# A macaron transformer block on one core: the turn between attention and the second feed-forward part, with its score steps in pairs, and the last statistics at other steps

## The chip, the cores and the metric

The kernel runs on one core of a Trainium2 chip. The metric is the device time of one execution in microseconds (us), as the median of the runs shown. A profile is one further execution, recorded by the hardware; its clock starts at the start of its span.

The engines are PE (TensorE, matmuls and transposes), PEld (its weight loads), DVE (VectorE), ACT (ScalarE), POOL (GpSimd) and SP (SyncE, here only DMA issues). Each works through its own list in order.

## The reference: what is computed

The input is 16 sequences of 256 tokens with 256 features, in float32. Three parts follow one another, each on a layernorm of x and added to x:

```
x = x + 0.5 * ffn(layernorm(x))       # 256 -> 1024, exact gelu, 1024 -> 256, weights
                                      # rounded to -1, 0, 1 by the mean of their sizes
x = x + attn(layernorm(x))            # 16 heads of 16 features, rotary, causal softmax
x = x + 0.5 * ffn(layernorm(x))       # the same weights as in the first part
```

## The kernel before

**Feed-forward.** x stays on the chip as eight blocks of 512 tokens (`xs[0..7]`, four tiles of 128 tokens each; sequence b is tiles 2b and 2b+1, so block b // 2). `ffn` (line 273) makes a part with `ln` = 0 or 2. Its unit is a step (`step`, line 373), of which there are 8 for each block i, one for each f of 128 hidden features, and `LATE` = 2 more at the end. A step u = 8i + f does `up(i, f)`: four matmuls from `xnT` into a PSUM tile "m" (`up_first`, unless made earlier), two gelus on ACT (`h_high`, rounded, and `h_whole`), and their difference `h_rest`, which POOL makes for f = 1, 3, 5 and DVE for the others. Then it does `down` for the step two earlier: eight matmuls with `h_high` and `h_rest` into a PSUM tile "w". At f = 3 DVE normalizes the next block (`prepare`, not for i = 0 of the last part), at f = 5 and 6 that is transposed (`turn_in`: four transposes into a PSUM tile "mm", a copy on ACT to the rounded half of `xnT`, a subtraction on DVE for the other half), and at f = 6 POOL adds the output bias to the block (`add_bias`). After f = 7's `down`, DVE adds the result to x, and SP stores the block.

**Attention.** A sequence b goes through eight slots p of two heads each. `scores` (line 505) makes scores in two forms: those of the sequence before, keys by queries, into a tile "w" (they become probabilities), and those of the current one, queries by keys, into tiles "m" or "w", from which DVE takes each row's maximum. A head uses 32 rows of PE's array, rows 32 * (h % 4), so the two heads of a slot take two of its four row groups; the other form uses slot p ^ 1 and so the other two. `scores` returns `weigh` (line 557): DVE adds the causal mask to "w", and ACT makes `pT`, its exp. `attend` multiplies four groups of heads by the values, ACT copies the result to `avs`; `divide` transposes that and divides by the sums on DVE (`o`); `turn_out` transposes `o` and copies it (`oT`); `project_out` multiplies by the output weights; `add_out` adds to x on DVE; `last_stats` (line 640) makes the layernorm statistics of the sequence's two tiles: four instructions on DVE (`st`, `mv`, twice) and two on POOL (`var`, `rstd`). `turn_max` transposes the maxima, copies them (`mT`) and sends them into `qT` by two DMAs of SP.

**The turn** (lines 745 to 797) is what the change touches. Sequences 13, 14 (called a) and 15 (z) are then still on their way: the scores of z have to be made, without other scores beside them, and the first two blocks of the last part are made ready at the same time. `prepare(1, gpsimd)` normalizes block 1 on POOL, `turn_in(1, 0)` and `turn_in(1, 1)` transpose it, and four `up_first` of block 0 run early. What remains of z (`tail`) stands behind the first steps of the last part, one item after each step.

**What sets the order.** All instructions of an engine run in the order in which the program issues them (`InOrder`, line 159; so every instruction of the compute engines shows line 167 in the profile). The order is written out by hand: `ahead` is issued between a slot's scores and its `weigh`, `behind` after it. PSUM is divided into three pools of two buffers each: "w" (two banks a buffer, one slot's scores of two heads), "m" and "mm" (one bank each). All transposes, `attend`, `project_out` and the projections use "mm".

Of the kernel before, what the change touches and what calls it, by code (L numbers as in the profile page):

```python
# [19 lines left out]
NFC = FF // P  # L20
# [9 lines left out]
def kernel(  # L30
# [15 lines left out]
    NB = NT // S  # L46
# [54 lines left out]
    for k in range(KC):  # L101
        rows = slice(k * P, (k + 1) * P)
        nc.sync.dma_start(out=wv[:, k, :], in_=wqkvT[rows, 2 * D :])
        for at in range(0, 2 * D, 4 * HD):
            n, j, e = at // D, at // P % 2, at // (4 * HD) % 2
# [53 lines left out]
    class InOrder:  # L159
# [11 lines left out]
    tensor, vector, scalar, gpsimd, sync = (  # L171
        InOrder(engine) for engine in (nc.tensor, nc.vector, nc.scalar, nc.gpsimd, nc.sync)
    )
# [4 lines left out]
    def stats(ln, n):  # L178
        st = small.tile([P, 6], FP, name="st")
        vector.bn_stats(st, tokens(n))  # L180
        vector.bn_aggr(mv[ln][:, n, :], st)
# [312 lines left out]
    def turn_max(b, j):  # L494

        tp = ps_mm.tile([P, S], FP, name="mm")
        for c in range(2):
            tensor.transpose(tp[:, c * P : (c + 1) * P], maxes[b % 2][:, c, j, :], ident)
        mT = hp.tile([P, S], FP, name="mT")
        scalar.copy(mT, tp)  # L500
        for e in range(2):
            rows = slice(HD * (1 - e), P, 32)
            sync.dma_start(out=qT[b][rows, 2 * j + e, :], in_=mT[rows, :])

    def scores(bw, pw, bm, pm):

        w = m = None  # L510
        if bw is not None:
            w = ps_w.tile([P, 2, 512], FP, name="w")
        if bm is not None and bw is None:
            both = ps_w.tile([P, 2, 512], FP, name="w")
            m = [both[:, j, :] for j in range(2)]
        elif bm is not None:
            m = [ps_m.tile([P, 512], FP, name="m") for j in range(2)]
        for c in range(2):
            for j in range(2):
                if w is not None:  # L520
                    h = 2 * pw + j
                    rows, g = slice(32 * (h % 4), 32 * (h % 4) + 32), h // 4
                    tensor.matmul(
                        w[:, j, c * S : S + c * P],
                        kT[bw][rows, g, c * P : (c + 1) * P],
                        qT[bw][rows, g, c * P : S],
                        start=(c == 0),
                        stop=(c == 1),
                    )
                if m is not None:  # L530
                    h = 2 * pm + j
                    rows, g = slice(32 * (h % 4), 32 * (h % 4) + 32), h // 4
                    tensor.matmul(
                        m[j][:, c * P : c * P + (c + 1) * P],
                        qT[bm][rows, g, c * P : (c + 1) * P],
                        kT[bm][rows, g, 0 : (c + 1) * P],
                        start=(c == 0),
                        stop=(c == 1),
                    )
        if m is not None:  # L540
            for j in range(2):
                h = 2 * pm + j
                at = 32 * (h % 4) + HD * (1 - h // 4 % 2)
                for c in range(2):
                    cols = (c + 1) * P
                    vector.tensor_tensor_reduce(
                        out=pp.tile([P, S], FP, name="masked")[:, 0:cols],
                        in0=m[j][:, c * P : c * P + cols],
                        in1=mask_q[:, S - cols : S],
                        scale=-1.0,  # L550
                        scalar=-MASKED,
                        op0=ALU.add,
                        op1=ALU.min,
                        accum_out=maxes[bm % 2][:, c, h // 8, at : at + 1],
                    )

        def weigh():

            at = w.rearrange("p h (d w) -> p h d w", w=2 * P)[:, :, :, 0:P]
            mask = mask_k.unsqueeze(1).unsqueeze(1).to_broadcast([P, 2, 2, P])  # L560
            vector.tensor_add(at, at, mask)

            pT[bw, pw] = prp.tile([P, 2, S + P], FP, name="pT")
            scalar.activation(pT[bw, pw], w[:, :, 0 : S + P], AF.Exp, scale=HD**-0.5)

        return weigh if w is not None else lambda: None

    def attend(b, half, take=True):


        av = ps_mm.tile([P, 2, S], FP, name="mm")
        for n in range(2):
            g = 2 * half + n
            for c in range(2):
                for r in range(4):
                    tensor.matmul(
                        av[32 * r : 32 * r + 32, n, c * P : S],
                        vals[b % 2][:, c, 4 * g + r, :],
                        pT[b, 2 * g + r // 2][:, r % 2, c * S : S + c * P],
                        start=(c == 0),  # L580
                        stop=(c == 1),
                    )
        sums[b, half] = av
        if take:
            take_sums(b, half)

    def take_sums(b, half):
        av, sums[b, half] = sums[b, half], pp.tile([P, 2, S], FP, name="avs")
        scalar.copy(sums[b, half], av)

    def divide(b, half):

        if half == 0:
            o[b] = pp.tile([P, 2, H, HD], FP, name="o")
        tp = ps_mm.tile([P, 2, 8, 32], FP, name="mm")
        for c in range(2):
            for n in range(2):
                tensor.transpose(
                    tp[:, c, 4 * n : 4 * n + 4, :].rearrange("p h d -> p (h d)"),
                    sums[b, half][:, n, c * P : (c + 1) * P],  # L600
                    ident,
                )
        inv = pp.tile([P, 2, 8, 1], FP, name="inv")
        vector.reciprocal(inv, tp[:, :, :, HD : HD + 1])
        vector.tensor_mul(
            o[b][:, :, 8 * half : 8 * half + 8, :],
            tp[:, :, :, 0:HD],
            inv.to_broadcast([P, 2, 8, HD]),
        )

    def turn_out(b):
        tp = ps_mm.tile([P, KC, S], FP, name="mm")
        for k in range(KC):
            for c in range(2):
                tensor.transpose(
                    tp[:, k, c * P : (c + 1) * P],
                    o[b][:, c, 8 * k : 8 * k + 8, :].rearrange("p h d -> p (h d)"),
                    ident,
                )
        oT[b] = pp.tile([P, KC, S], FP, name="oT")  # L620
        scalar.copy(oT[b], tp)

    def project_out(b):
        y = y_a[b] = ps_mm.tile([P, 2, D], FP, name="mm")
        for c in range(2):
            for k in range(KC):
                tensor.matmul(
                    y[:, c, :],
                    oT[b][:, k, c * P : (c + 1) * P],
                    wo[:, k, :],  # L630
                    start=(k == 0),
                    stop=(k == KC - 1),
                )

    def add_out(b):
        at = 2 * b % BT
        xt = xs[2 * b // BT][:, at : at + 2, :]
        vector.tensor_add(xt, y_a[b], xt)

    def last_stats(b):  # L640
        for c in range(2):
            stats(2, 2 * b + c)
        finish_stats(2, 2 * b, 2)
# [101 lines left out]
    begin, step, prepare, turn_in, up_first = ffn(2, store)  # L745
    rest = []
    for p in range(8):
        made = []
# [9 lines left out]
    a, z = NB - 2, NB - 1  # L758


    ahead = {
        0: lambda: project_out(NB - 3),
        1: lambda: turn_max(z, 1),
    }
    behind = {
        0: lambda: (add_out(NB - 3), prepare(1, gpsimd)),
        2: lambda: attend(a, 1),
        3: lambda: (up_first(0, 0), made.append(turn_in(1, 0))),
        4: lambda: (made.pop()(), divide(a, 1), up_first(0, 1)),
        5: lambda: (turn_out(a), made.append(turn_in(1, 1))),  # L770
        6: lambda: (made.pop()(), attend(z, 0)),
        7: lambda: (project_out(a), divide(z, 0), add_out(a)),
    }
    for p in range(8):
        weigh = scores(z, p, None, None)
        ahead.get(p, lambda: None)()
        weigh()
        behind.get(p, lambda: None)()

    more = ps_w.tile([P, 2, TB], FP, name="w")  # L780
    for f in range(2):
        up_first(0, 2 + f, more[:, f, :])
    tail = [
        lambda: attend(z, 1, False),
        lambda: take_sums(z, 1),
        lambda: divide(z, 1),
        lambda: turn_out(z),
        lambda: project_out(z),
        lambda: add_out(z),
        lambda: last_stats(NB - 3),  # L790
        lambda: last_stats(a),
        lambda: last_stats(z),
    ]
    for u in range(FFN_STEPS):
        step(u)
        if u < len(tail):
            tail[u]()
# [49 lines left out]
```

## Time and profile before

| | us |
|---|---|
| median of three runs | 623.5 (623.47 to 624.73) |
| the profiled execution | 623.6 |
| its span | 621.8 |
| PE busy | 600.7 (97%) |
| DVE busy | 462.1 (74%) |
| ACT busy | 415.3 (67%) |
| POOL busy | 306.4 (49%) |
| the turn, from the end of slot 7 of z to attend(z, 1) | 466.3 to 487.9 |
| the last feed-forward part behind it | to 621.8 |

The granted clock of PE was 0.998 of full speed. Lines of the timeline give the start, the duration, the engine, the operation with its tiles (output<-inputs) and shapes, and in brackets the idle time of the engine before it and who ended it. Equal neighbours are merged (x4). Matmuls are pipelined: the ends of PE's rows are modelled, and starts tell more. A matmul in float32 leaves two records.

### The profile page before, as it was taken

The page shows a single profiled execution, that of the slowest core. Times are in us where ns is not written, and L with a number is a line of the kernel's source. Part 1 is how long each engine was busy: PE and PEld are TensorE (multiplying, and loading weights), DVE is VectorE, ACT ScalarE, POOL GpSimd, SP SyncE. Part 2 cuts the span into 40 slices and gives each one's busy share as a digit, 9 for nine tenths or more (in the row PEclk, how much of TensorE's full clock was granted, in tenths as well). Part 3 has the DMA queues.
Part 4 walks back from the last instruction along what each step waited for, and adds up shares of the span by engine and source line. Part 5 has one row for each costly group of instructions (what it writes and reads, how often), then busy time and mean ns, then how long its engine had stood idle before and what let it go on. Part 6 is the DMA issues. An engine that isn't in the chain of part 4 may idle for free.

```text
span 621.8 us, 14721 instructions
## 1 busy us (share of the span) xinstructions
PE 600.7 (97%) x5580; PEld 487.5 (78%) x5580; DVE 462.1 (74%) x1650; ACT 415.3 (67%) x716; POOL 306.4 (49%) x277
## 2 busy tenths in 40 slices
PE   4999999999999999999999999999999999999997
PEld 3798999887667777777777777777766788888886
DVE  6877777785788888888888888888885375555553
ACT  4666766674576667776777677767765666676674
POOL 3655555782464455545564456553442163334443
PEclk9999999999999999999999999999999999999999
DMA  9800000000001000110010001100100011011001
GB/s 286 178 21 1 2 1 18 17 1 18 20 35 38 18 22 35 37 36 21 19 37 36 20 20 36 37 19 21 36 4 2 1 35 35 34 35 35 26 21 56
DMA packets 25478, 21.30 MB, mean 34 GB/s; under 512 B 10944, under 2 KB 21056, under 8 KB 25408
## 3 DMA queue, kind: packets, MB, share of 16 engines
q1 hardware_dynamic: 24848, 19.44, 9.9%
q8 instruction: 44, 0.72, 0.5%
q10 hardware_dynamic: 560, 0.92, 0.4%
q14 instruction: 26, 0.21, 0.1%
HBM read 7.51 MB, written 4.19 MB: 19 GB/s over the span
## 4 chain that ended last, share of the span: by engine, by line
PE 87%; DVE 7%; ACT 2%; issue 2%; POOL 1%; DMA 1%; DVEq 0%; ACTq 0%; POOLq 0%
PE mm L167 37%; PE w L167 28%; PE m L167 21%; DVE h_rest L167 2%; DVE st L167 1%; DVE xn L167 1%; ACT h_high L167 1%; ACT h_whole L167 1%; DVE w2q L167 1%; DMA x<-in_x_dram 1%; DVE mv L167 1%; DVE masked L167 0%; DVE x L167 0%; POOL h_rest L167 0%; POOL rstd L167 0%
## 5 line engine op out<-in xcount | busy, mean ns | idle before, releaser
L167 DVE CUSTOM_DVE_ANT_0 masked<-m,mask_q 128x128 f32<-128x128 f32 x480 | 142.7, 353 | 41.0 <-PE m L167 39.7
L167 PE MATMUL m<-xnT,w1q 128*128 128x512 f32 x504 | 142.5, 404 | 0.9 <-DVE w1q L167 0.9
L167 ACT ACTIVATE h_high<-m,b_sb 128x512 fp32r<-128x512 f32 x126 | 86.7, 688 | 79.2 <-PE m L167 79.2
L167 DVE TENSOR_TENSOR h_rest<-h_whole,h_high 128x512 fp32r<-128x512 f32 x83 | 76.1, 918 | 71.0 <-ACT h_whole L167 70.6
L167 ACT ACTIVATE pT<-w 128x768 f32<-128x768 f32 x128 | 104.1, 814 | 31.6 <-DVE w L167 24.6
L167 PE MATMUL w<-qT,kT 32*128 32x256 f32 (+1 forms) x1024 | 121.7, 349 | 0.8 <-ACT pT L167 0.5
L167 POOL TENSOR_TENSOR h_rest<-h_whole,h_high 128x512 fp32r<-128x512 f32 x45 | 60.3, 1340 | 125.7 <-ACT h_whole L167 125.5
L167 PE MATMUL w<-w2q,h_high 128*128 128x256 f32 x480 | 120.9, 286 | 1.1 <-DVE w2q L167 1.1
L167 PE MATMUL w<-w2q,h_rest 128*128 128x256 f32 x480 | 118.0, 280 | 1.3 <-POOL h_rest L167 1.2
L167 PEld LDWEIGHTS w<-qT,kT 32*128 32x128 f32 x1024 | 90.7, 184 | 32.4 <-issue 26.4
L167 PE MATMUL m<-kT,qT 32*128 32x128 f32 x960 | 114.9, 349 | 0.7 <-ACT kT L167 0.7
L167 PEld LDWEIGHTS m<-xnT,w1q 128*128 128x128 f32 x504 | 86.7, 190 | 16.4 <-DVE xnT L167 2.9
L167 PEld LDWEIGHTS w<-w2q,h_rest 128*128 128x128 f32 x480 | 90.6, 189 | 6.4 <-POOL h_rest L167 1.8
L167 PEld LDWEIGHTS w<-w2q,h_high 128*128 128x128 f32 x480 | 90.4, 188 | 5.8 <-DVE w2q L167 1.6
L167 DVE TENSOR_TENSOR w<-w,mask_k 128x512 f32<-128x512 f32 x128 | 88.9, 695 | 7.1 <-PE w L167 7.1
L167 ACT ACTIVATE h_whole<-m,b_sb 128x512 f32<-128x512 f32 x126 | 85.8, 681 | 0.0
L167 PEld LDWEIGHTS m<-kT,qT 32*128 32x128 f32 x960 | 65.9, 185 | 2.9 <-ACT kT L167 1.6
L167 POOL TENSOR_TENSOR w<-w,cosT 128x512 f32<-128x512 f32 x32 | 41.2, 1289 | 51.9 <-ACT w L167 32.0
L167 PE MATMUL mm<-xnT_a,wqk 128*128 128x256 f32 x256 | 62.2, 386 | 0.0
L167 POOL TENSOR_TENSOR w<-w,sinT 128x512 f32<-128x512 f32 x32 | 40.9, 1278 | 25.7 <-DMA w<-w 25.6
L167 PEld LDWEIGHTS mm<-xnT_a,wqk 128*128 128x128 f32 x256 | 46.2, 190 | 7.6 <-issue 0.7
L167 PE MATMUL mm<-pT,vals 128*32 128x256 f32 (+1 forms) x1024 | 48.2, 329 | 0.3 <-ACT oT L167 0.3
(90 smaller groups left out, 888.0 us busy)
## 6 DMA issues: line engine op xcount, KB each, us to landing
w<-w SPq DMA_DIRECT2D x64, 128.0 KB
out_dram<-x SPq DMA_DIRECT2D x15, 256.0 KB
x<-in_x_dram SPq DMA_DIRECT2D x7, 512.0 KB
w<-in_w2T_dram SPq DMA_DIRECT2D x1, 1024.0 KB
qT<-mT SPq DMA_DIRECT2D x64, 4.0 KB
w<-in_w1T_dram SPq DMA_DIRECT2D x1, 512.0 KB
w<-in_w1T_dram ACTq DMA_DIRECT2D x1, 512.0 KB
wqk<-in_wqkvT_dram SPq DMA_DIRECT2D x16, 32.0 KB
```

The costliest lines, as they stand in the source:

```text
L167: return tc.keep_in_program_order(getattr(self.engine, name)(*args, **kwargs))
```

## The change

In the turn, z's eight score slots are issued in four pairs. For each pair both slots' scores come first, and then both `weigh`. A pair holds the heads 2p to 2p + 3, so its four heads lie on the four row groups of PE. The work between the slots is put in another order: `project_out(13)` and the first `up_first` go ahead of all scores, attend(a, 1) and the second `up_first` behind the first pair, `divide(a, 1)`, `turn_in(1, 0)` and `turn_out(a)` behind the second, attend(z, 0) and `turn_in(1, 1)` behind the third, the rest behind the fourth. `add_out(13)` now stands behind two `weigh` instead of one.

In the tail, the statistics of sequences 13, 14 and 15 move from behind the steps u = 6, 7 and 8 to behind u = 12, 20 and 28, that is behind f = 4 of blocks 1, 2 and 3. No instruction is added or removed.

```diff
-    ahead = {
-        0: lambda: project_out(NB - 3),
-        1: lambda: turn_max(z, 1),
+    project_out(NB - 3)
+    up_first(0, 0)
+    ahead = {0: lambda: turn_max(z, 1)}
+    behind = {
+        0: lambda: (add_out(NB - 3), prepare(1, gpsimd), attend(a, 1), up_first(0, 1)),
+        2: lambda: (divide(a, 1), made.append(turn_in(1, 0)), turn_out(a)),
+        4: lambda: (made.pop()(), attend(z, 0), made.append(turn_in(1, 1))),
+        6: lambda: (made.pop()(), project_out(a), divide(z, 0), add_out(a)),
     }
-    behind = {
-        0: lambda: (add_out(NB - 3), prepare(1, gpsimd)),
-        2: lambda: attend(a, 1),
-        3: lambda: (up_first(0, 0), made.append(turn_in(1, 0))),
-        4: lambda: (made.pop()(), divide(a, 1), up_first(0, 1)),
-        5: lambda: (turn_out(a), made.append(turn_in(1, 1))),
-        6: lambda: (made.pop()(), attend(z, 0)),
-        7: lambda: (project_out(a), divide(z, 0), add_out(a)),
-    }
-    for p in range(8):
-        weigh = scores(z, p, None, None)
+    for p in range(0, 8, 2):
+        both = [scores(z, p + n, None, None) for n in range(2)]
         ahead.get(p, lambda: None)()
-        weigh()
-        behind.get(p, lambda: None)()
+        for weigh in both:
+            weigh()
+        behind[p]()
...
-        lambda: last_stats(NB - 3),
-        lambda: last_stats(a),
-        lambda: last_stats(z),
     ]
+    for b in (NB - 3, a, z):
+        tail += [lambda: None] * (-(len(tail) + 4) % NFC) + [lambda b=b: last_stats(b)]
```

## The prediction

> All clock times below are microseconds (us) from the start of the span of the profiled execution. **Names:** a is sequence 14, z is sequence 15; "z4" is the score step of heads 8 and 9 of z; (i, f) is step f of block i in the last feed-forward part, u = 8i + f.
>
> **What bounds the kernel now.** First the page's shares of the chain that ended last:
>
> ```profile
> PE 87%; DVE 7%; ACT 2%; issue 2%; POOL 1%; DMA 1%; DVEq 0%; ACTq 0%; POOLq 0%
> ```
>
> TensorE sets the time, except for small gaps; so I ask only where PE stands still. The table of stretches shows two such places around the change: PE is busy 20.62 of the 21.60 us of the turn (466.3 to 487.9) and 2.16 of the 3.00 us from 508 to 511. From 511 to 607 it has no gap by this measure: 15.98 or 15.99 of every 16. What delays PE there by less than a gap is seen only in the timeline.
>
> The turn, from its timeline (columns: start, duration, engine, operation, idle before it and who ended that):
>
> ```profile
> 468.26 1.29 DVE L167 TENSOR_TENSOR w<-w,mask_k 128x512 f32<-128x512 f32 x2
> ...
> 469.90 0.69 DVE L167 TENSOR_TENSOR x<-mm,x 128x512 f32<-128x512 f32 x1 [0.35 <-POOL xn L167]
> ...
> 469.93 0.92 PE L167 MATMUL w<-qT,kT 32*128 32x256 f32 x8
> ...
> 480.72 0.58 ACT L167 COPY oT<-mm 128x512 f32<-128x512 f32 x1
> ...
> 481.35 1.51 PE L167 MATMUL mm<-pT,vals 128*32 128x256 f32 x32 [0.31 <-ACT oT L167]
> ```
>
> Read three things. Two masks on DVE take 1.29 together: about 0.60 from one start to the next, however fast PE makes scores. `add_out(13)` (x<-mm,x) comes when its product ends (469.8; the name POOL in the bracket is only the last semaphore). And attend(z, 0) at 481.35 waits for the copy of oT: "mm" has two buffers taken in turn, and attend got that of turn_out(a). So a tile "mm" can't be written before the tile two before it was read. In the new order this rule bites, as worked out below.
>
> The first steps of the last part, on POOL, then on DVE:
>
> ```profile
> 507.76 0.19 POOL L167 TENSOR_SCALAR var<-mv 128x2 f32<-128x2 f32 x1 [0.34 <-DVE mv L167]
> 508.04 0.70 POOL L167 TENSOR_TENSOR rstd<-var,power 128x2 f32<-128x2 f32 x1
> 508.70 1.27 POOL L167 TENSOR_TENSOR h_rest<-h_whole,h_high 128x512 fp32r<-128x512 f32 x1
> ```
>
> ```profile
> 507.49 0.18 DVE L167 BATCH_NORM_AGGREGATE mv<-st 128x2 f32<-128x6 f32 x1
> ...
> 508.78 1.74 DVE L167 TENSOR_TENSOR h_rest<-h_whole,h_high 128x512 fp32r<-128x512 f32 x1
> ```
>
> POOL's h_rest (1,1) could have run at 506.67 (its h_whole ended at 506.64) but stood behind var and rstd of z's statistics. PE waited for it: up(1,3) starts at 507.97 and up(1,4) at 510.96, 2.99 where a plain step takes 1.87. Those 1.12 us are what the statistics cost today. Note also the second row of DVE: asked 0.07 after POOL had begun, an h_rest of DVE (0.69 alone) lasts 1.74, to 0.55 after POOL's end. It stood still while POOL worked.
>
> A steady block (2), DVE, POOL, PE:
>
> ```profile
> 529.48 0.69 DVE L167 TENSOR_TENSOR h_rest<-h_whole,h_high 128x512 fp32r<-128x512 f32 x1 [1.75 <-ACT h_whole L167]
> 531.83 0.69 DVE L167 TENSOR_TENSOR xnT<-mm,xnT 128x512 fp32r<-128x512 f32 x1 [1.65 <-ACT xnT L167]
> 533.66 1.96 DVE L167 TENSOR_TENSOR h_rest<-h_whole,h_high 128x512 fp32r<-128x512 f32 x1 [1.14 <-ACT h_whole L167]
> 535.54 0.68 DVE L167 TENSOR_TENSOR xnT<-mm,xnT 128x512 fp32r<-128x512 f32 x1
> ```
>
> ```profile
> 531.40 1.29 POOL L167 TENSOR_TENSOR h_rest<-h_whole,h_high 128x512 fp32r<-128x512 f32 x1 [2.45 <-ACT h_whole L167]
> 532.65 2.42 POOL L167 TENSOR_TENSOR x<-x,b_sb 128x1024 f32<-128x1024 f32 x1
> ```
>
> ```profile
> 533.53 1.09 PE L167 MATMUL m<-xnT,w1q 128*128 128x512 f32 x4
> ...
> 535.40 1.37 PE L167 MATMUL m<-xnT,w1q 128*128 128x512 f32 x4
> ```
>
> Here is the chain without slack. POOL's h_rest of f=5 and its bias addition run back to back to 535.06. DVE's h_rest of f=6, asked at 533.66, stands until 535.06 and ends 0.55 later, at 535.61. Behind it on DVE is the second xnT subtraction (to 536.22), and the fourth matmul of the next block's first step waits for that: 1.37 instead of 1.09, and the step lasts 2.14 instead of 1.87 from start to start. So any delay of POOL at f=5 goes to PE whole.
>
> **The change, part by part.**
>
> *1. The turn in pairs.* Removed on PE: side by side, 16 records on four row groups took about as long (463.27 to the next instruction at 464.24) as 8 on two (0.85 to 0.92). Four pairs instead of eight slots would save 4 x 0.85 = 3.4 us of PE. But what ends last in the new order is DVE and the buffers of "mm". Step by step:
>
> - project_out(13) starts after slot 7, about 466.35, and takes 1.83 (483.64 to 485.47): 468.2. up_first(0,0), about 1.0: 469.2; its xnT is ready at 467.24 and its buffer "m" at 467.8. z0 starts, and z1 must wait for the exp of the slot before, which nothing moves: 469.93, as today. Both end at 470.8: only up_first(0,0) is gained.
> - add_out(13) now stands on DVE behind the masks of z0 and z1: masks to 471.6, add_out 471.6 to 472.3. attend(a,1) takes the "mm" buffer of that product: 472.3, while PE was free at 471.15 (turn_max 0.36). A stall of 1.15. attend 1.44: 473.75; up_first(0,1) and the switch to 32 rows 1.1: 474.9.
> - z2 and z3 side by side 0.9: 475.8. Masks at 475.95 and 476.55, reciprocal 477.15, multiplication 477.45 to 477.87. PE does divide's and turn_in's transposes (0.45 each) and then waits about 1.2 for o: turn_out(a) at 477.93. With 0.53 (479.59 to 480.12 today): 478.46.
> - z4 and z5: 479.36. Masks at 479.55 and 480.15, xnT subtraction 480.75 to 481.43. attend(z,0) takes the buffer of turn_in(1,0), which that subtraction reads: 481.49, a stall of 2.1. It ends at 482.93; turn_in 0.53: 483.46.
> - z6 and z7: 484.36, where today all of this is done at 483.64. project_out(a): 486.2; divide(z,0) waits for the second subtraction (masks 484.55 and 485.15, subtraction to 486.43): 486.49, today 485.47.
> - ACT: the two last exps 485.99 to 486.80 (today to 485.36), table load 1.28, four gelus to 490.53 (today 489.09), then z's avs at 490.54 for 489.50, h_rest (0,2) at 492.33 for 491.28, and turn_out(z), which waits behind it, at 493.7 for 492.65.
>
> **Turn: +1.05.** From below: if none of the "mm" waits came, the saved PE time less the w buffers' waits would stand, about -3; from above, with every stall 0.15 longer, +1.6. The DMAs of turn_max go out at 471.66 as today (mT's copy comes no earlier), and z4 reads them 2.6 later than today; SP has nothing else then. POOL's prepare(1) still starts at 465.05 when xn is free and ends at 469.87, long before its turn_in at 476.2.
>
> The 0.9 for a pair is read off the set at 463.27, where an m record of 256 columns (463.60) starts before the w records of 128 columns that stand ahead of it in the program (463.81): row groups overtake each other. Serial, a pair would take 1.7. Even then the odd slot's mask, today 0.19 after its scores, starts at the same time as in the chain above, since the even one's mask runs meanwhile; only project_out(a) would come later, +0.3 in all. The Trainium skill ("TensorE: Matmul & The Clock Gate", Part 3, The mechanism) says that matmuls start and end strictly in program order; by it the second slot would begin only behind the first one's last records, and the sum would be up to 0.3 higher. The row at 463.60 contradicts it for starts.
>
> *2. Statistics out of u = 6, 7, 8.* h_rest (1,1) runs at its time, with 1.0 to spare: **-1.1** (2.99 - 1.87). The 0.2 lost at 503.1 stays, for it comes from the bias addition of block 0. Bounds: -0.9 and -1.35.
>
> *3. Statistics into f=4 of blocks 1, 2, 3.* On DVE they fit: after h_rest at 529.48 (+0.61) four instructions of 1.16 in all (503.18 to 504.34) run from 530.09 to 531.25, ahead of the subtraction at 531.83. On POOL they don't. From the start of the second mv to the start of the h_rest behind rstd took 1.21 (507.49 to 508.70), with DVE off SBUF pairs as it will be here. The second mv starts at 530.09 + 0.98 = 531.07, so h_rest (2,5) starts at 532.29 instead of 531.40. PE doesn't need it before 534.6. But the bias addition behind it moves from 532.65 to 533.54, and so stays 0.12 ahead of DVE's h_rest (2,6), asked at 533.66. DVE then stands until 535.95, the subtraction ends at 537.1, and PE's fourth matmul comes 0.89 later than today. Blocks 1 and 3 give the same lead (their f=4 h_rest at 513.40 and 545.58, f=6 at 517.57 and 549.75: 4.17 apart each time). **3 x 0.89 = +2.7.** Below: were DVE first, its h_rest would end at 534.35, the present wait of 0.27 would go too, and each block would give -0.27. Above: 3 x 1.0.
>
> POOL, 0.07 ahead at 508.70, kept DVE out for its whole duration. The Trainium skill ("SBUF — State Buffer", SBUF: two separate sides) says that the first to start gets it for the whole instruction; a lead of 0.12 would then suffice, but which of the two gets it when both wait at an instruction's end, it doesn't say.
>
> **Sum:** 623.6 (profiled execution: span 621.8 and 1.8 around it) + 1.05 - 1.1 + 2.7 = 626.2. The median of the runs shown is 0.1 lower: 626.1.
>
> **Rivals.**
> - *DVE wins the port* in blocks 1 to 3. For it: the lead is 0.12 us, and a var of 0.54 (504.43) instead of 0.19 would turn it. Against: var took 0.54 only beside an h_rest of DVE. Time: 623.5 + 1.05 - 1.1 - 0.8 = 622.6. If one or two blocks flip: 623.8 to 625.
> - *The pairs pay* (the other side). PE saves its 3.4 in the turn because the waits for "mm" aren't there, the masks keeping up as today. Place: attend(a,1) and attend(z,0); it decides if the stalls there together are under 1 instead of 3.3. For it: PE is 95% busy in the turn. Against: the wait at 481.35. Time: 623.5 - 3 - 1.1 + 2.7 = 622.1.
> - *The scores aren't side by side* (the change doesn't do what it says): 626.4.
>
> **How the numbers follow.** A measurement can tell about 0.2% (1.25 us) from no change. Forecast 0.61 (with the serial pairs), own range 624.6 to 627.8; one or two blocks flipping 0.13; DVE first in all three 0.16; pairs paying 0.10. Faster (below 622.25): half of the last and part of the one before, 0.13. Within: the flips, most of DVE first and a little of the forecast, 0.26. Slower 0.61. The range goes from 622.4 to 627.8.
>
> **What would show it.** In the profile after: PE stalls before attend(a,1) (about 1.1, DVE x), turn_out(a) (1.2, DVE o) and attend(z,0) (2.1, DVE xnT); up(1,3) to up(1,4) 1.87 apart; DVE's h_rest of f=6 at 2.85 instead of 1.96 and the block's first step about 3.0 long in blocks 1 to 3, and 2.14 in blocks 4 to 6. Wrong if attend follows the transposes at once, or if h_rest of f=6 takes 0.69 there.

## The result and the profile after

| us | before | after |
|---|---|---|
| median | 623.5 (22 runs) | 624.28 (22 runs) |
| span of the profiled execution | 621.8 | 622.5 |
| PE busy in the turn, 466.3 to 487.9 (21.6) | 20.62 | 18.94 |
| PE busy, 508 to 511 (3.0) | 2.16 | 3.00 |
| PE busy, each 16 us from 511 to 559 | 15.99, 15.98, 15.99 | 15.06, 15.06, 15.06 |

The ratio to before is 1.0014, with a 95% interval of 1.0008 to 1.0021: slower, but by a third of what was forecast. Two parts of opposite sign make this sum, as the first experiments will show. The chain of the page hardly differs:

```profile
PE 86%; DVE 7%; ACT 3%; issue 2%; DMA 1%; POOL 1%; DVEq 0%; SPq 0%; POOLq 0%; ACTq 0%
```

The turn after, from its timeline over all engines (start, duration, engine, operation, and in brackets the idle time before it and who ended it):

```profile
470.61 1.30 DVE L167 TENSOR_TENSOR w<-w,mask_k 128x512 f32<-128x512 f32 x2 [1.62 <-PE w L167]
...
471.29 0.37 ACT L167 COPY mT<-mm 128x256 f32<-128x256 f32 x1 [1.38 <-PE mm L167]
...
471.71 1.51 PE L167 MATMUL mm<-pT,vals 128*32 128x256 f32 x32 [0.46 <-ACT mT L167]
471.81 0.68 DVE L167 TENSOR_TENSOR x<-mm,x 128x512 f32<-128x512 f32 x1
...
477.37 0.63 PE L167 MATMUL mm<-ident,o 128*128 128x128 f32 x4 [1.13 <-DVE o L167]
...
478.80 1.51 PE L167 MATMUL mm<-pT,vals 128*32 128x256 f32 x32
...
480.17 0.68 DVE L167 TENSOR_TENSOR xnT<-mm,xnT 128x512 fp32r<-128x512 f32 x1
...
480.90 0.66 PE L167 MATMUL mm<-ident,xn 128*128 128x128 f32 x4 [0.59 <-DVE xnT L167]
```

The wait for o at 477.37 is there as forecast (1.13 for 1.2). The other two aren't. attend(a, 1) starts at 471.71, 0.10 before add_out(13) (x<-mm,x) even begins; what it waited for is mT, the copy of turn_max's tile. And attend(z, 0) at 478.80 waits for nothing, though the subtraction comes at 480.17; it is the next tile, turn_in(1, 1), that waits for that.

What the turn gains is read where the next regular step begins, at up(0, 4). PE, before and then after:

```profile
492.85 1.19 PE L167 MATMUL m<-xnT,w1q 128*128 128x512 f32 x4
```

```profile
491.97 1.17 PE L167 MATMUL m<-xnT,w1q 128*128 128x512 f32 x4
```

A changed block, number 1: POOL, DVE, and PE's first step of the block after it:

```profile
513.23 0.19 POOL L167 TENSOR_SCALAR var<-mv 128x2 f32<-128x2 f32 x1 [2.39 <-DVE mv L167]
513.50 0.72 POOL L167 TENSOR_TENSOR rstd<-var,power 128x2 f32<-128x2 f32 x1
514.20 1.29 POOL L167 TENSOR_TENSOR h_rest<-h_whole,h_high 128x512 fp32r<-128x512 f32 x1
515.45 2.42 POOL L167 TENSOR_TENSOR x<-x,b_sb 128x1024 f32<-128x1024 f32 x1
```

```profile
515.54 2.88 DVE L167 TENSOR_TENSOR h_rest<-h_whole,h_high 128x512 fp32r<-128x512 f32 x1 [1.14 <-ACT h_whole L167]
518.34 0.68 DVE L167 TENSOR_TENSOR xnT<-mm,xnT 128x512 fp32r<-128x512 f32 x1
```

```profile
517.28 0.85 PE L167 MATMUL m<-xnT,w1q 128*128 128x512 f32 x3
519.07 0.50 PE L167 MATMUL m<-xnT,w1q 128*128 128x512 f32 x1 [0.94 <-DVE xnT L167]
...
520.35 0.86 PE L167 MATMUL m<-xnT,w1q 128*128 128x512 f32 x3
```

The bias addition begins 0.09 before DVE asks for h_rest; DVE stands for its whole 2.42; the subtraction is late, and PE has three of four matmuls done and waits 0.94. The steps from one `up` to the next at the block's end (517.28 to 520.35 here; it is the first step of the block after) are 3.07, 3.06 and 3.06 for blocks 1 to 3, and 2.14, 2.13 and 2.12 for blocks 4 to 6. From up(1,3) to up(1,4) it is 1.87 now.

### The profile page after: what moved, and what is told of

It is laid out like the page before. It is cut to its first block, busy times and chain, and to the rows that moved or that the text cites. A ratio compares the mean times of both kernels' runs of the same rounds, so it can differ in the third digit from the quotient of the medians.

```text
span 622.5 us, 14719 instructions
## 1 busy us (share of the span) xinstructions
PE 598.3 (96%) x5580; PEld 485.2 (78%) x5580; DVE 462.5 (74%) x1650; ACT 415.1 (67%) x716; POOL 305.3 (49%) x277
## 4 chain that ended last, share of the span: by engine, by line
PE 86%; DVE 7%; ACT 3%; issue 2%; DMA 1%; POOL 1%; DVEq 0%; SPq 0%; POOLq 0%; ACTq 0%
PE mm L167 37%; PE w L167 28%; PE m L167 21%; DVE h_rest L167 2%; ACT h_high L167 1%; ACT h_whole L167 1%; DMA w<-in_w1T_dram 1%; DVE xn L167 1%; DVE xnT L167 1%; DVE w2q L167 1%; DVE st L167 0%; DVE x L167 0%; DVE masked L167 0%; DVE w L167 0%; DVE mv L167 0%
## 5 line engine op out<-in xcount | busy, mean ns | idle before, releaser
L167 DVE TENSOR_TENSOR h_rest<-h_whole,h_high 128x512 fp32r<-128x512 f32 x83 | 77.8, 939 | 73.8 <-ACT h_whole L167 73.4
L167 PE MATMUL w<-qT,kT 32*128 32x128 f32 (+1 forms) x1024 | 118.5, 349 | 0.1
L167 PEld LDWEIGHTS w<-qT,kT 32*128 32x128 f32 x1024 | 88.5, 184 | 30.5 <-issue 25.9
```

Source lines behind the costliest of these rows:

```text
L167: return tc.keep_in_program_order(getattr(self.engine, name)(*args, **kwargs))
```

## The experiments

**The two halves alone.** `turn_only` takes the changed kernel and puts the three `last_stats` back behind u = 6, 7, 8; `tail_only` takes the kernel before and moves only them.

```diff
# turn_only, against the changed kernel
+        lambda: last_stats(NB - 3),
+        lambda: last_stats(a),
+        lambda: last_stats(z),
-    for b in (NB - 3, a, z):
-        tail += [lambda: None] * (-(len(tail) + 4) % NFC) + [lambda b=b: last_stats(b)]
```

> The new turn with the old tail (statistics behind u = 6, 7, 8). Theory 1 (the turn gains, the tail loses): up(0,4) starts at 492.0 as in the changed kernel, 0.8 earlier than before, and POOL's h_rest (1,1) waits behind rstd again: 623.5 - 0.85 = 622.65. Theory 2 (the turn costs the 1.05 of the forecast and something else gave it back): 624.5.

> The old turn with the new tail (statistics behind u = 12, 20, 28). Theory 1: the loss in blocks 1 to 3 belongs to the step alone: three block steps of 3.06 instead of 2.14, and 1.12 saved at u = 11: 623.5 - 1.12 + 2.76 = 625.15. Theory 2 (the loss comes from the phase that the new turn gives): 622.4.

Measured: turn_only 622.49 (0.9983 of before, 0.9975 to 0.9992), tail_only 625.17 (1.0028, 1.0018 to 1.0037), before 623.46 beside them. So the turn gains 0.97 and the tail loses 1.71; their sum, +0.74, is close to the 0.78 of the whole change. In turn_only's trace up(1,3) to up(1,4) lasts 3.00 again; in tail_only's the three block ends last 3.06 to 3.07. The loss belongs to the tail alone, the gain to the turn alone, and theory 1 holds for both.

**Where the statistics stand.** One step later:

```diff
-        tail += [lambda: None] * (-(len(tail) + 4) % NFC) + [lambda b=b: last_stats(b)]
+        tail += [lambda: None] * (-(len(tail) + 3) % NFC) + [lambda b=b: last_stats(b)]
```

> The changed kernel with the statistics behind f = 5 instead of f = 4 of the same blocks (u = 13, 21, 29). Theory 1 (the loss is the port: whoever of DVE and POOL starts first): var and rstd now stand between POOL's h_rest and the bias addition, so DVE's h_rest (i,6) starts before the bias addition and lasts 0.7 instead of 2.85; the first step after each of the three blocks is 1.87 instead of 3.06: 624.28 - 3 x 1.19 = 620.7. Theory 2 (the loss is the work of the statistics on DVE and POOL between two steps, wherever it stands): no change, 624.3 (within 0.5), or later by up to 1, since the DVE part now stands closer to the end of the block.

Measured 620.64 (0.9951 of before, 0.9939 to 0.9964): theory 1 to the tenth. POOL, then DVE, in the same block:

```profile
513.22 1.30 POOL L167 TENSOR_TENSOR h_rest<-h_whole,h_high 128x512 fp32r<-128x512 f32 x1 [2.43 <-ACT h_whole L167]
515.51 0.72 POOL L167 TENSOR_SCALAR var<-mv 128x2 f32<-128x2 f32 x1 [0.99 <-DVE mv L167]
516.31 0.72 POOL L167 TENSOR_TENSOR rstd<-var,power 128x2 f32<-128x2 f32 x1
517.01 2.44 POOL L167 TENSOR_TENSOR x<-x,b_sb 128x1024 f32<-128x1024 f32 x1
```

```profile
515.24 0.18 DVE L167 BATCH_NORM_AGGREGATE mv<-st 128x2 f32<-128x6 f32 x1
515.49 0.69 DVE L167 TENSOR_TENSOR h_rest<-h_whole,h_high 128x512 fp32r<-128x512 f32 x1
516.10 0.68 DVE L167 TENSOR_TENSOR xnT<-mm,xnT 128x512 fp32r<-128x512 f32 x1
517.80 2.80 DVE L167 TENSOR_TENSOR h_rest<-h_whole,h_high 128x512 fp32r<-128x512 f32 x2 [1.02 <-ACT h_whole L167]
```

The same instructions do the same work. But var and rstd now hold the bias addition back until 517.01, DVE's h_rest of f = 6 takes 0.69, and this time it is var that is held (0.72 for 0.19). The bias addition holds the next h_rest, of f = 7 (the two merged at 517.80 take 2.80), which has a step to spare. All three block ends last 1.87.

**Whoever waits at the end of an instruction.** `stats_twice` makes POOL late enough for DVE's request to fall into POOL's h_rest, with the bias addition queued directly behind:

```diff
         finish_stats(2, 2 * b, 2)
+        if b >= NB - 3:
+            finish_stats(2, 2 * b, 2)
```

> The changed kernel with var and rstd of the last three sequences computed twice on POOL (the output stays the same). POOL's h_rest (i,5) starts about 1.0 later (515.2 instead of 514.25 in the clock of the changed kernel's profile) and is still running when DVE asks for h_rest (i,6); the bias addition is queued directly behind it. If DVE, waiting, gets the port at POOL's instruction boundary: DVE's h_rest ends about 0.6 after POOL's h_rest, the step after the block is about 1.9, and the time falls to 624.3 - 3 x 1.1 = 621. If POOL keeps it: the step is about 4.0 and the time 624.3 + 3 x 1.0 = 627.2.

Measured 621.83 (0.9972, 0.9961 to 0.9983). POOL, then DVE:

```profile
515.14 1.29 POOL L167 TENSOR_TENSOR h_rest<-h_whole,h_high 128x512 fp32r<-128x512 f32 x1
516.40 2.86 POOL L167 TENSOR_TENSOR x<-x,b_sb 128x1024 f32<-128x1024 f32 x1
```

```profile
515.44 1.55 DVE L167 TENSOR_TENSOR h_rest<-h_whole,h_high 128x512 fp32r<-128x512 f32 x1 [1.14 <-ACT h_whole L167]
516.91 0.68 DVE L167 TENSOR_TENSOR xnT<-mm,xnT 128x512 fp32r<-128x512 f32 x1
```

DVE, waiting since 515.44, goes at POOL's instruction end (516.43) and ends 0.56 later; the bias addition, though next in POOL's list, is held and lasts 2.86 for 2.42. PE:

```profile
516.25 0.28 PE L167 MATMUL w<-w2q,h_high 128*128 128x256 f32 x1
516.49 0.39 PE L167 MATMUL w<-w2q,h_rest 128*128 128x256 f32 x1
...
517.41 1.08 PE L167 MATMUL m<-xnT,w1q 128*128 128x512 f32 x4
...
519.27 1.09 PE L167 MATMUL m<-xnT,w1q 128*128 128x512 f32 x4
```

The first step after the block lasts 1.86 (517.41 to 519.27), as the first branch expected. A new loss stands one step earlier: `down` of f = 7 multiplies by the h_rest of f = 5, which POOL now ends only at 516.43, so its second matmul starts 0.24 behind the first instead of 0.12, and the step of f = 7 lasts 2.09, 2.08 and 2.08 in the three blocks instead of 1.87. That is 0.64 in all. With three block ends of 1.87 instead of 3.06 this makes 624.28 - 3.57 + 0.64 = 621.35, close to the profiled execution (621.30); why the median lies 0.5 above that (runs from 621.15 to 622.50), the one trace doesn't show. More work on POOL made the kernel 2.4 faster than the changed one.

**The bias addition elsewhere.** First behind f = 7, in the changed kernel:

```diff
-                if f == (1 if i == NBLK - 1 else 6):
+                if f == (1 if i == NBLK - 1 else 7 if ln == 2 else 6):
```

> The changed kernel with the bias addition of the last part behind f = 7 instead of f = 6 (blocks 0 to 6), statistics still behind f = 4. Theory 1 (port): DVE's h_rest (i,6) isn't held in any block: three steps of 3.06 and three of 2.14 become 1.87, and 0.2 of block 0 go: 624.28 - 3 x 1.19 - 3 x 0.27 - 0.2 = 619.7. The h_rest (i,7) is held instead, which has a step of slack. Theory 2 (POOL's lateness itself, not the port): h_rest of f = 5 is as late as before, so the three blocks stay at 3.06 and the time near 624.

Measured 624.14 (1.0007, 0.9999 to 1.0016): a miss, and it tells nothing between the theories. POOL in block 3:

```profile
548.03 1.29 POOL L167 TENSOR_TENSOR h_rest<-h_whole,h_high 128x512 fp32r<-128x512 f32 x1
549.28 2.41 POOL L167 TENSOR_TENSOR x<-x,b_sb 128x1024 f32<-128x1024 f32 x1
556.64 1.30 POOL L167 TENSOR_TENSOR h_rest<-h_whole,h_high 128x512 fp32r<-128x512 f32 x1 [4.95 <-ACT h_whole L167]
```

POOL has nothing to do between the h_rest of f = 5 and that of f = 1 in the next block, and the addition waits for nobody. Moved past two steps of the program it moved past no instruction of its own engine, and runs exactly where it ran. So the next run puts it where POOL's own list orders it, between the h_rest of f = 3 and that of f = 5, on top of the statistics behind f = 5:

```diff
-                if f == (1 if i == NBLK - 1 else 6):
+                if f == (1 if i == NBLK - 1 else 4 if ln == 2 else 6):
...
-        tail += [lambda: None] * (-(len(tail) + 4) % NFC) + [lambda b=b: last_stats(b)]
+        tail += [lambda: None] * (-(len(tail) + 3) % NFC) + [lambda b=b: last_stats(b)]
```

> The kernel with the statistics behind f = 5, and the bias addition of the last part behind f = 4, so that on POOL it stands between h_rest of f = 3 and h_rest of f = 5 (behind f = 7 it had moved in the program only: POOL has nothing between f = 5 and f = 1 of the next block, so it ran at the same time). Theory 1 (port): DVE's h_rest (i,4) is held instead, which has about 0.8 to spare, and h_rest (i,6) in no block: the steps behind blocks 4 to 6 fall from 2.14 to 1.87 and that behind block 0 loses its 0.2: 620.64 - 3 x 0.27 - 0.2 = 619.6. Theory 2 (the 0.27 at the end of a block is not the port's): 620.6, or later if the late h_rest (i,4) pushes DVE's row of subtraction, statistics and h_rest (i,6).

Measured 619.52 (0.9934, 0.9921 to 0.9948), theory 1. DVE in block 3:

```profile
542.74 2.39 DVE L167 TENSOR_TENSOR h_rest<-h_whole,h_high 128x512 fp32r<-128x512 f32 x1 [1.68 <-ACT h_whole L167]
545.08 0.69 DVE L167 TENSOR_TENSOR xnT<-mm,xnT 128x512 fp32r<-128x512 f32 x1
...
549.22 0.69 DVE L167 TENSOR_TENSOR h_rest<-h_whole,h_high 128x512 fp32r<-128x512 f32 x1 [1.02 <-ACT h_whole L167]
```

The hold is still there, but on the h_rest of f = 4, where nothing of PE's hangs on it. Every block end from 0 to 6 lasts 1.87: the 0.27 that blocks 4 to 6 lost already before were the same hold.

**Is it PE's time that the turn gains?** `same_rows` pairs slots whose heads lie on the same row groups, so that nothing of a pair runs side by side:

```diff
     for p in range(0, 8, 2):
-        both = [scores(z, p + n, None, None) for n in range(2)]
+        q = p if p % 4 == 0 else p - 1
+        both = [scores(z, q + 2 * n, None, None) for n in range(2)]
```

> The changed kernel with the pairs made of slots p and p + 2, whose heads lie on the same two row groups of PE, so that a pair takes about 1.7 instead of 0.9 us. Theory 1 (DVE sets the pace of the pairs: 0.6 per mask, and PE has stalls to spare behind the second and third pair): the time that the scores need on PE is mostly free, as the forecast had it: +0.3 to +0.8, 624.6 to 625.1. Theory 2 (the turn gains because PE is the bound there and the pair saves it 0.8 each time): three pairs x 0.8 = +2.4, 626.7.

Measured 624.76 (1.0023, 1.0015 to 1.0032), 0.48 more than the changed kernel (0.62 if each is set against the kernel before that ran beside it). PE after this edit:

```profile
474.44 1.58 PE L167 MATMUL w<-qT,kT 32*128 32x256 f32 x16
475.94 0.66 PE L167 MATMUL mm<-ident,avs 128*128 128x128 f32 x4
...
477.59 0.63 PE L167 MATMUL mm<-ident,o 128*128 128x128 f32 x4 [0.56 <-DVE o L167]
```

A pair now holds PE for 1.50 (474.44 to 475.94) instead of 0.88 (474.27 to 475.15 in the changed kernel), and the wait for o shrinks from 1.13 to 0.56 in return. Three such pairs take PE 1.9 longer, and 0.5 to 0.6 of that reaches the end. So theory 1: behind a pair PE waits for DVE, and time saved on PE is mostly waited away. Half of the turn's gain of 0.9 to 1.0, or somewhat more, is thus the pairs' running side by side. The rest is put down to the new order of the work between the scores by subtraction; no run has that order alone with single slots.

**Which buffer a new tile gets.**

```diff
-    ahead = {0: lambda: turn_max(z, 1)}
+    ahead = {}
     behind = {
-        0: lambda: (add_out(NB - 3), prepare(1, gpsimd), attend(a, 1), up_first(0, 1)),
+        0: lambda: (add_out(NB - 3), prepare(1, gpsimd), attend(a, 1), turn_max(z, 1), up_first(0, 1)),
```

> The changed kernel with turn_max(z, 1) behind attend(a, 1) instead of ahead of it. Theory 1 (a new tile mm takes the buffer whose last reader stands earliest in the program: attend(a, 1) got that of turn_max and waited 0.46 for the copy mT): attend now gets the buffer of turn_in(0, 1), long free, and starts when the scores end, about 470.8 instead of 471.7; turn_max gets the buffer of project_out(13) and waits for add_out(13), which ends at 472.5, beside attend's 1.4 us: the later steps come up to 0.4 earlier, 623.9. Theory 2 (the two buffers strictly in turn): the same start, but then attend(a, 1) should have waited for add_out in the changed kernel, and it didn't. Against a gain: mT goes out about 1.9 later, and if its DMA lands after 477.5, the third pair waits for it.

Measured 623.83 (1.0001, 0.9992 to 1.0010), 0.45 less than the changed kernel (0.31 if each is set against the kernel before that ran beside it). PE:

```profile
469.23 1.32 PE L167 MATMUL w<-qT,kT 32*128 32x256 f32 x16
470.48 1.51 PE L167 MATMUL mm<-pT,vals 128*32 128x256 f32 x32
472.30 0.41 PE L167 MATMUL mm<-ident,maxes 128*128 128x128 f32 x2 [0.32 <-DVE x L167]
```

attend(a, 1) follows the scores at once, and it is turn_max that now waits for add_out (DVE x): it got the buffer of project_out(13), two tiles back and next to be free in the program's order. These waits fit both theories; what tells them apart are the rows of the changed kernel above, where attend(a, 1) starts before add_out and attend(z, 0) before the subtraction. Whether the choice goes by the last reader's place in the program or by when that reader is expected to end, no run separates. The DMAs that go out later are in nobody's way: the third pair follows turn_out(a) without a wait.

**All together.** `bias_max` joins max_later to bias_eighth, `sixth_max` to stats_sixth, and `all_three` to bias_fifth; no further edit.

> The two edits together: bias addition behind f = 7 and turn_max behind attend(a, 1). If they are independent, 619.7 - 0.4 = 619.3, or 0.6% below the kernel before.

> Statistics behind f = 5 and turn_max behind attend(a, 1), bias addition as in the changed kernel. If the two gains are independent (turn and blocks lie apart in time, PE the bound behind both): 620.64 - 0.45 = 620.2.

> Statistics behind f = 5, bias addition behind f = 4, turn_max behind attend(a, 1). If all are independent: 619.6 - 0.45 = 619.15, 0.7% below the kernel before.

Measured: bias_max 623.80 (1.0005, 0.9997 to 1.0014), a miss, which is max_later alone, as the edit of bias_eighth changes nothing; sixth_max 620.20 (0.9946, 0.9934 to 0.9959); all_three 619.15 (0.9931, 0.9919 to 0.9944). The gains add up as expected, within what these runs can tell, and all_three is the fastest kernel of the study, 4.3 below the kernel before beside it (623.46).

## Why the prediction was right or wrong

The sign was right and the size wrong: 626.1 was forecast, 624.28 came. The sign came right only because the term of blocks 1 to 3 outweighs the others; the turn's own sign was wrong. By the terms of the sum:

- **Turn, forecast +1.05, measured -0.88** (up(0,4) starts at 491.97 instead of 492.85; -0.97 in turn_only's time). This term failed, by 1.9 us, all that the forecast is off. The step that failed is "a tile 'mm' can't be written before the tile two before it was read". From one row (attend(z, 0) waits for oT) I took the two buffers to alternate. That row agrees as well with another rule, which all waits read here fit: a new tile takes the buffer whose last reader stands earliest in the program. Where tiles are read in the order in which they were made, the two are the same. They differ where a read stands late: add_out(13), and the subtraction, which the program holds back in `made`. There a later tile had been read before, so attend(a, 1) got turn_max's buffer (0.46 of waiting instead of 1.15) and attend(z, 0) that of turn_out(a) (none instead of 2.1). The subtraction's wait went to turn_in(1, 1), 0.59. Together these waits are 1.05 where the forecast had 3.25. The stall of 2.1 before attend(z, 0), which the prediction had named as what would show it right, isn't there.
- **In the turn, what held:** z1 as late as before, the wait for o at turn_out(a) (1.13 for 1.2), the wait at divide(z, 0) (0.20 for about 0.3), the pair at 0.88 for 0.9, and that the pace is DVE's. The bound of -3 "if none of the mm waits came" and the rival *the pairs pay* at 622.1 were wrong in size because of that pace: the stalls at the two attends did stay under the 1 us that it named, and it still paid 0.9 and not 3. One start was also wrong: project_out(13) begins at 466.72 and not 466.35, since its "mm" buffer is read by a subtraction until then (0.28 <-DVE xnT); the wait of z1 took that up.
- **u = 11, forecast -1.1, measured -1.12:** 2.99 to 1.87, back at 3.00 in turn_only.
- **Blocks 1 to 3, forecast 3 x 0.89 = +2.7, measured 3 x 0.92 = +2.8:** the lead of the bias addition (0.12 forecast, 0.09 measured), the hold (2.88 for 2.85) and the stall were as worked out. tail_only gives +1.71 for this and the term before.
- The rival *DVE wins the port* didn't come, but it was not far: in stats_sixth, with the statistics one step of the program later, DVE starts first, and in stats_twice, with 1 us more on POOL, DVE waits for one POOL instruction only.

The sum of the measured terms, -0.88 - 1.12 + 2.76 = +0.76, is the difference of the medians, 0.78.

## What to carry to other kernels

A step of another engine that looks free is priced by what is queued behind it, on its own engine first: the statistics fitted into DVE's idle time, and cost 2.8 us because they pushed a POOL instruction of 2.4 us that shuts DVE out, and the DVE chain behind it had no slack. Before pricing a wait for a buffer, list who reads each tile and where that read stands in the program; one observed wait may fit two rules of reuse. And an instruction moved in the program moves in time only if it passes another one of its own engine, or gets something to wait for: bias_eighth took 624.14 for 624.28.

## What the runs showed of the hardware that was not expected

When DVE and POOL both want the way to SBUF that they share, the first to start keeps it, even by 0.09 us (after); that the Trainium skill says too ("SBUF — State Buffer", SBUF: two separate sides). In stats_sixth 0.02 to 0.04 sufficed the other way round, for DVE's h_rest against POOL's var. What that section leaves open, stats_twice shows: at the end of POOL's instruction the waiting DVE goes first, even against a POOL instruction that is queued directly behind (bias addition 2.86 instead of 2.42), in each of the three blocks. In bias_fifth it is the same one step earlier: POOL's h_rest of f = 5, directly behind the bias addition for which DVE's h_rest of f = 4 waits, lasts 1.63 instead of 1.29 in blocks 1 to 6.

Even a POOL instruction of 0.19 us on 128 x 2 elements is held by DVE's h_rest (var 0.72 in stats_sixth).

Scores that stand one whole slot later in PE's list still overlap: 16 records on four row groups take 0.88 us, 8 on two took 0.85.
